# Earlier lists for the experts' middle groups, and a new order of measuring, scaling and routing inside the attention rounds

## The chip, the cores and the metric

The kernel runs on one core of one Trainium2 chip. The metric is the device time of one execution in microseconds (us). An execution's own time is a little longer than the span of its profile, which runs from the first to the last recorded instruction.

## The reference

One layer of a gated cross-attention model, in float32, for 8 batches of 512 rows of 256 numbers:

```python
x = x + tanh(g_xattn) * xattn(layernorm(x), ctx, mask)   # 16 heads of 16
x = x + tanh(g_ffn) * moe(layernorm(x))

# moe, over all 4096 rows
probs = softmax(x @ router_w + router_b)                 # 8 experts
top_w, top_idx = top_k(probs, 2)
output = sum over e: comb[:, e] * (gelu(x @ up[e].T) @ down[e].T)    # 1024 hidden
```

The mask excludes keys. Its rows are all alike here and leave a run of at most 128 adjacent keys, which the kernel finds out at run time before it branches to this variant. Only two of the eight experts count for a row.

## The kernel before

**Engines.** TensorE (PE) multiplies and transposes, VectorE (DVE) reduces and does small arithmetic, ScalarE (ACT) does Exp, Gelu and copies out of PSUM, GpSimd (POOL) issues indirect gathers and scatters, SyncE (SP) issues the other transfers. The code is written as Python functions ("steps") that emit a few instructions each; a scheduler then fixes the order on each engine by its own estimates, except that the instructions marked `tc.keep_in_program_order` ("pinned") stay in the written order among themselves. Each engine, and each engine's queue of transfers, works in that order. An instruction that waits holds what is behind it.

**Start.** The mask and `x` of batch 0 are loaded, batch 0 is measured (`measure`, L211: `look` makes mean and variance of the four 128-row tiles with `bn_stats` and `bn_aggr`, L225 and L228; `settle`, twelve small DVE operations, L233 to L246, makes 1/sqrt of the variance in three Newton steps and the shift). The window of keys is found from the mask; SP loads its start into a register and then issues the windows of context (L508), `x` of batch 1 and the small tensors. `near_i` (L609) is what the branch reads.

**Attention rounds.** The loop at L1198 goes over b = -1 to 7. In round b the attention weights of batch b are computed, the scores' maxima ("tops") of batch b + 1 are found, batch b - 1 is projected, normalized and routed to experts, and batches b + 2 and b + 3 are prepared. A round has four parts g (half of the heads by parity each) of three steps n, and `between(old=b-1, new=b+2, next_=b+3)` (L1114) makes a plan: a list of steps for each (g, n). In order, a part runs `weights_T` (w_ps L1058 on PE, Exp to n_pT L1063 on ACT), then `weigh` of the part before (n_av L1076, DVE raw L1082 and so on), `find_tops` (t_ps L1028 on PE, tops L1033 on DVE), `lower_tops` (top_ps L1046, ql L1047), with the plan's steps between them. The plan's steps that matter here:

- `looks` and `settle` of `measure`, for the rows of the expert part (job "f") and the next batch's attention (job "a").
- `scale` (L275): four ACT operations that make the normalized rows xn_f or xn_a. Only the first of four was pinned. `turn` (L285, L286) transposes them.
- `keys_values` (kv_ps L539, kn L543, nv L544), `keys_T` (k_ps L551, k L557), `keys_less`, `queries` (q_ps L570).
- `logits` (route_ps L323, lgT L328) in the last part of a round. In the next round `route` (L330) transposes lgT (lg_ps L332), adds the bias (L334), and goes on to the softmax, the two best experts and their weights (Exp at L341; both L360). `place` (L363: place_ps L368, then small POOL operations) counts the rows of each expert, and eight `enter` scatters (L398) write a batch's entries into a table in memory.

**Expert groups.** The sorted rows are computed in 32 groups of 256 (and a few beyond). `list_rows(s)` (L800) loads the line of group s into a register on SP and fetches its lists from the table (L806). `load(s)` (L811) issues the expert's weights up (L816) and down (L817), 1024 KB each, into one of three buffers. `fetch(s)` gathers the rows (xg L826), `turn` transposes them, `go_up` does 32 matrix multiplications h_ps (L874) and the Gelus (hT L878), `go_down` 32 of o_ps (L892), and adds to what was gathered of the output (y L895), which POOL scatters back (L898). `SIZES` is [5, 12, 4, 18]: groups 0 to 4 are planned after batch 3's entries, groups 5 to 16 after batch 6's, the rest at the end. Groups 0 to 3 are computed inside rounds 5 to 7 (the table `amid`), groups 4 to 31 in the main loop (`compute`, L914), which runs list_rows(s + 4) and load(s + 2) with group s:

```python
for s in range(DONE, MAIN):
    for step in compute(s, MAIN, DONE):
        step()
        if queue:
            queue.popleft()()
```

`queue` holds what is left of batches 6 and 7: projection, logits, `route`, `place` and scatters. Banks of PSUM: two ("g") for kv_ps, k_ps, q_ps, proj_ps, top_ps, lg_ps, route_ps, place_ps and o_ps, five ("s") for t_ps, w_ps and h_ps, one for n_av.

Of the kernel before, what the change touches and what calls it, by code (L numbers as in the profile page):

```python
# [16 lines left out]
ALU = mybir.AluOpType  # L17
AX = mybir.AxisListType
# [50 lines left out]
def flamingo_layer(ctx: ExitStack, tc: tile.TileContext, a: dict, out: bass.AP):  # L69
# [190 lines left out]
    def shared(p2, small, bank):  # L260
        def layernorms(jobs, pin=False, measured=None):


            said, looks, settle_all = measured or measure(small, [job[:2] for job in jobs], pin)
            settle = lambda pin=False: settle_all(pin)

            def own(k):
                b, which, dst = jobs[k]

                def scale(ts):  # L270
                    if ts[0] == 0:
                        said[k] = p2.tile([P, QT, D], F32, tag="xn", name=f"xn_{which}_{b}")
                    for t in ts:
                        at = k * QT + t
                        ins = nc.scalar.activation(  # L275
                            said[k][:, t, :], xs[b][:, t, :], AF.Identity,
                            bias=said["shift"][:, at : at + 1], scale=said["rstd"][:, at : at + 1],
                        )
                        if t == ts[0] and pin:
                            tc.keep_in_program_order(ins)  # L280

                def turn(c):
                    ps = bank(f"xnT_ps_{which}_{b}_{c}")
                    for t in range(QT):
                        nc.tensor.transpose(ps[:, t * P : (t + 1) * P], said[k][:, t, c * P : (c + 1) * P], ident)  # L285
                    nc.scalar.copy((dst() if callable(dst) else dst)[:, c, :], ps)  # L286
# [14 lines left out]
        def finish(b):  # L301
# [28 lines left out]
            def route():  # L330
                ps = bank(f"lg_ps{b}")[:, :P]
                nc.tensor.transpose(ps, said["lgT"], ident)  # L332
                lg = t3("lg")
                nc.vector.tensor_tensor(  # L334
                    lg, ps.rearrange("p (t e) -> p t e", t=QT)[:, :, :E], over_t(rb), ALU.add
                )
                mx = t2("mx")
                nc.vector.tensor_reduce(mx, lg, AX.X, ALU.max)
                nc.vector.tensor_tensor(lg, lg, over_e(mx), ALU.subtract)
# [64 lines left out]
            places = [place] + [lambda t=t: enter(t) for t in range(b * QT, (b + 1) * QT)]  # L404
            return x2T, keep_x, keep_rows, logits, route, places

# [42 lines left out]
    with early, tc.tile_pool(name="ps_mask", bufs=1, space=PSUM) as ps_mask:  # L449
# [23 lines left out]

        norms_0 = measure(const, [(0, "a")], True)
        settle_0 = norms_0[2]
# [39 lines left out]
        win = load_window(mk, 0)  # L515
        load_x(1, pin=True)
        wins = {1: load_window(const, 1, pin=True)}
# [90 lines left out]
        nc.vector.scalar_tensor_tensor(near, uneven, 0.0, near, ALU.is_le, ALU.mult)  # L608
        tc.keep_in_program_order(nc.vector.tensor_copy(near_i, near))  # L609
        drop = column("drop", P)  # L610
        tc.keep_in_program_order(nc.vector.tensor_scalar(drop, row_ps, -1.0, 1.0, ALU.mult, ALU.add))
# [8 lines left out]

        keep_ones(vals[0])
        for t in vals[1:]:
            keep_ones(t)
# [5 lines left out]
    def experts(pool, seen, half_bank, bank, row_bank):  # L629
# [283 lines left out]

        def compute(s, end, first):  # L914

# [13 lines left out]
            else:  # L929

                steps += up[:2] + last + up[2:]
            if s + 4 < end:
                steps.append(lambda: list_rows(s + 4))
# [34 lines left out]
    def attend_near(att):  # L968
# [136 lines left out]

        def normalize(*jobs):
            looks, settle, each = layernorms(jobs, True)
            for job, own in zip(jobs, each):
                normal[job[:2]] = own
            return looks, settle  # L1110

        def between(old, new, next_):
# [9 lines left out]
            if old is not None:  # L1122
                x2T, keep_x, keep_rows, logits, route, place = finish(old)
                jobs.append((old, "f", x2T))
# [5 lines left out]
            if new is not None:  # L1130
# [4 lines left out]
                if new == 1:  # L1135
                    put(1, 1, *turns)
                    put(2, 1, keys_T)
                    put(3, 1, queries[0])
                    put(3, 2, queries[1], keys_less)
                else:  # L1140
                    put(1, 1, *turns, keys_T)
                    put(3, 0, keys_less)
                    put(2, 0, queries[0])
                    put(2, 1, queries[1])
# [6 lines left out]
            if next_ is not None:  # L1151
                put(*((2, 2) if old is None else (0, 2)), looks[-1])
            if old is not None:
# [4 lines left out]
            if jobs:  # L1158
                put(*((3, 1) if old is None else (1, 2)), settle)
            if old is not None:  # L1160
                put(2, 0, *scales)
                put(2, 2, lambda: keep_rows(rows_f()))
                put(3, 0, *turns)
                put(3, 1, logits)
                place, *enter = place
                counts = [count for count, end in zip(plans, PARTS) if old + 1 == end]
                later.append((route, place, enter, counts))
            return plan


        def begin():
# [75 lines left out]
        wait = lambda: None  # L1247
        (route, place, enter, _), (route_last, last, enter_last, counts) = later
        mixed = [step for pair in zip(rest, [route, place, *enter] + [wait] * len(rest)) for step in pair]
        spread = [step for one in enter_last for step in (one, wait, wait)]  # L1250
        queue = deque([*mixed, route_last, last, *spread, *counts])
        for s in range(DONE, MAIN):
            for step in compute(s, MAIN, DONE):
                step()
# [9 lines left out]
    def attend_anywhere(att):  # L1264
# [143 lines left out]
        def end(b):  # L1408
            x2T, keep_x, keep_rows, logits, route, place = finish(b)
            (look,), settle, ((normal, scales, turns),) = layernorms([(b, "f", x2T)])  # L1410
            return [keep_x, look, settle, *scales, lambda: keep_rows(normal()), *turns, logits, route, *place]

# [178 lines left out]
```

## Time and profile before

| What | us |
|---|---|
| median of 9 executions | 813.44 (812.07 to 818.64) |
| the profiled execution, its own time | 811.85 |
| its span | 810.1 |
| PE busy in the span | 751.5 |
| first w_ps of rounds 0 to 7 | 37.0, 62.05, 98.03, 136.10, 174.80, 213.52, 262.79, 307.40 |
| main loop alone on PE, about | 445 to 777 |

The profile is a record of one execution: for each engine the start and length of each instruction, what its engine waited for before it, and for PE the clock that was granted, as a share of full speed. The mean granted clock was 0.97. A line such as L1033 is a line of the kernel before. In lines of groups, "out<-in" are the names of the tiles that are written and read, with buffer numbers left out, and x16 counts instructions. "[1.59 <-PE row_ps L599]" says that the engine had been idle for 1.59 us and that the PE instruction of line 599 ended this.

### The profile page before, as it was taken

What the parts mean: (1) busy time and instruction counts of PE and PEld (TensorE: products, weight loads), DVE (VectorE), ACT (ScalarE), POOL (GpSimd) and SP (SyncE); (2) the same over time, 40 slices, a digit from 0 to 9 for tenths busy, and PEclk for the clock granted to TensorE, in tenths of its full rate; (3) what the DMA queues carried; (4) which work ended last, traced back from release to release, by engine and by line L of the source; (5) the groups of instructions that cost most, each with busy time, mean ns of one, the idle gap of its engine ahead of it and who ended that gap; (6) DMA issues with size and microseconds to landing.
All of it is one profiled execution on the core that took longest, in us unless ns stands there. A gap on an engine that the chain in (4) does not pass through costs nothing. (4 is left out here: it accounts for less than half of the span.)

```text
span 810.1 us, 11155 instructions
## 1 busy us (share of the span) xinstructions
PE 751.5 (93%) x3898; PEld 541.1 (67%) x3898; DVE 409.7 (51%) x1315; ACT 254.9 (31%) x487; POOL 312.0 (39%) x420
## 2 busy tenths in 40 slices
PE   8999987888999989998899999999999999999992
PEld 3444443434565756667678888888788788888872
DVE  8887895959664574533163353525343433523300
ACT  4563735454554434332312111111211211121110
POOL 2021115142627251546573534444443443344331
PEclk9998998999899999999999999999999999999997
DMA  5700201000573230143638566666744754654310
GB/s 163 265 7 8 78 34 56 27 30 28 193 263 121 81 121 14 54 158 115 227 125 294 192 215 219 204 224 192 243 164 152 227 195 151 203 202 174 100 53 25
DMA packets 82728, 113.32 MB, mean 140 GB/s; under 512 B 16605, under 2 KB 67552, under 8 KB 82656
## 3 DMA queue, kind: packets, MB, share of 16 engines
q1 hardware_dynamic: 70000, 85.16, 31.3%
q0 software_dynamic: 11840, 26.76, 9.9%
q8 instruction: 35, 0.57, 0.3%
q10 hardware_dynamic: 816, 0.53, 0.2%
q14 instruction: 37, 0.30, 0.1%
HBM read 92.66 MB, written 20.28 MB: 139 GB/s over the span
## 5 line engine op out<-in xcount | busy, mean ns | idle before, releaser
L892 PE MATMUL o_ps<-down,hT 128*128 128x256 f32 x1088 | 243.0, 381 | 4.3 <-DVE y L895 4.3
L874 PE MATMUL h_ps<-xT,up 128*128 128x256 f32 (+1 forms) x1024 | 242.7, 393 | 4.0 <-DVE xT L851 2.4
L892 PEld LDWEIGHTS o_ps<-down,hT 128*128 128x128 f32 x1088 | 205.8, 190 | 40.7 <-DVE y L895 6.3
L874 PEld LDWEIGHTS h_ps<-xT,up 128*128 128x128 f32 x1024 | 193.2, 190 | 46.7 <-issue 5.6
L863 DVE STREAM_TRANSPOSE xT<-xg 32x128 f32<-32x128 f32 (+1 forms) x368 | 115.6, 314 | 180.0 <-DMA xg<-rows,listed 165.0
L878 ACT ACTIVATE hT<-h_ps 128x512 f32<-128x512 f32 (+1 forms) x144 | 82.1, 573 | 347.7 <-PE h_ps L874 302.3
L898 POOL DMA_INDIRECT out<-y,listed x68 | 68.5, 1007 | 149.8 <-DVE y L895 131.4
L826 POOL DMA_INDIRECT y<-out,listed x68 | 64.9, 955 | 76.5 <-DMA out<-y,listed 49.4
L1033 DVE TENSOR_REDUCE tops<-t_ps 128x4 f32<-128x512 f32 x128 | 79.5, 683 | 20.5 <-PE t_ps L1028 17.1
L1063 ACT ACTIVATE n_pT<-w_ps 128x512 f32<-128x512 f32 x128 | 67.8, 597 | 48.5 <-PE w_ps L1058 45.1
L826 POOL DMA_INDIRECT xg<-rows,listed x68 | 66.1, 972 | 37.9 <-issue 18.6
L398 POOL DMA_INDIRECT table<-entries,place_i x64 | 63.0, 985 | 25.0 <-issue 16.5
L895 DVE SCALAR_TENSOR_TENSOR y<-o_ps,listed,y 128x256 f32<-128x256 f32 x68 | 31.3, 482 | 74.4 <-PE o_ps L892 50.2
L1058 PE MATMUL w_ps<-ql,km 32*128 32x512 f32 x256 | 52.7, 685 | 1.8 <-DVE tops L1033 1.4
L1010 POOL TENSOR_TENSOR x<-x,bo 128x1024 f32<-128x1024 f32 x8 | 18.8, 2354 | 72.4 <-DVE bo L1009 42.4
L1028 PE MATMUL t_ps<-k,q 32*128 32x256 f32 x512 | 44.5, 420 | 1.3 <-ACT n_pT L1063 0.9
L1082 DVE STREAM_TRANSPOSE raw<-n_av 128x512 f32<-128x512 f32 x32 | 22.8, 712 | 45.1 <-PE n_av L1076 28.3
L1028 PEld LDWEIGHTS t_ps<-k,q 32*128 32x128 f32 x512 | 27.4, 192 | 22.2 <-issue 8.2
L1076 PE MATMUL n_av<-n_pT,nv 128*32 128x512 f32 x256 | 38.7, 680 | 1.2 <-DVE xT L851 1.1
L1097 PE MATMUL proj_ps<-woT,oT 128*128 128x256 f32 x128 | 32.6, 397 | 0.0
L570 PE MATMUL q_ps<-n_xnT,wqT 128*128 128x512 f32 x64 | 31.4, 615 | 0.9 <-ACT n_xnT L286 0.6
L1097 PEld LDWEIGHTS proj_ps<-woT,oT 128*128 128x128 f32 x128 | 24.2, 196 | 9.7 <-issue 3.1
(220 smaller groups left out, 527.1 us busy)
## 6 DMA issues: line engine op xcount, KB each, us to landing
up<-in_upT SPq DMA_DIRECT2D x32, 1024.0 KB
down<-in_downT SPq DMA_DIRECT2D x32, 1024.0 KB
out<-x SPq DMA_DIRECT2D x8, 512.0 KB
rows<-xn_f SPq DMA_DIRECT2D x8, 512.0 KB
x<-in_x SPq DMA_DIRECT2D x7, 512.0 KB
table<-none SPq DMA_DIRECT2D x1, 2400.0 KB
xg<-rows,listed POOLq DMA_INDIRECT x68
y<-out,listed POOLq DMA_INDIRECT x68
```

Of the source, the lines that this page charges most:

```text
L398: nc.gpsimd.indirect_dma_start(out=table_parts[2 * t + i][:, :], out_offset=bass.IndirectOffsetOnAxis(ap=place_i[:, t, i : i + 1], axis=0) ...
L826: ins = nc.gpsimd.indirect_dma_start(out=dst, out_offset=None, in_=src[: seen[JOBS[s][0]], :], in_offset=bass.IndirectOffsetOnAxis(ap=list ...
L863: nc.vector.transpose(dst[32 * g : 32 * g + 32, i], src[32 * i : 32 * i + 32, g])
L874: nc.tensor.matmul(ps[:, i, :], lhsT=up[:, dc, (f + i) * P : (f + i + 1) * P], rhs=xT[:, dc, :], start=(dc == 0), stop=(dc == DC - 1),)
L878: nc.scalar.activation(made[s][:, f : f + m, :], ps, AF.Gelu)
L892: nc.tensor.matmul(ps, lhsT=hT[:, f, h * P : (h + 1) * P], rhs=down[:, f, :], start=(f == 0), stop=(f == FC - 1))
L898: ins = nc.gpsimd.indirect_dma_start(out=out_parts[h][:, :], out_offset=bass.IndirectOffsetOnAxis(ap=listed[:, n, h, 0:1], axis=0), in_=y[ ...
L1028: ins = nc.tensor.matmul(ps[j][:, u], lhsT=q[rows_j, c, t * P : (t + 1) * P], rhs=k[rows_j, c], start=True, stop=True)
L1033: nc.vector.tensor_reduce(top[:, 2 * tp : 2 * tp + 2, :].rearrange("p t (i x) -> p t i x", i=2)[:, :, :, 32 * j], ps[j], AX.X, ALU.max,)
L1058: ins = nc.tensor.matmul(ps[j], lhsT=km[rows_j, c, i, :], rhs=lowered[b, c][rows_j, i, :], start=True, stop=True)
L1063: nc.scalar.activation(pT[:, j, :], ps[j], AF.Exp)
L1097: nc.tensor.matmul(ps[:, t - ts[0], :], lhsT=outs[b, c][:, t * P : (t + 1) * P], rhs=w["woT"][:, c, :], start=(c == 0), stop=(c == DC - 1),)
```

## The change

It has six parts.

1. `x` of batch 1 is loaded before SP reads the window's start. Batch 1 is measured with batch 0's functions: its `look` stands right after `near_i`, its `settle` after the first `keep_ones`. It was measured at the begin of the rounds.
2. In round 0 the measurement of batch 3 goes from step (2, 2) to (1, 2), its `settle` from (3, 1) to (2, 0). In later rounds both stay where they were.
3. All four scalings of a job are pinned, not the first alone.
4. `route` is cut in two. The transpose and the addition stay in `route`, which goes from step (0, 2) to (0, 0); `choose`, the rest, stays at (0, 2), and its maximum is pinned.
5. `keys_T` goes from step (1, 1) to (1, 2).
6. The lists of groups 8 to 16 are asked for in the last step of round 7, after those of groups 6 and 7, and `compute` skips them; `turn_rows(4)` is moved one step by it.

```diff
@@ scale
-                        if t == ts[0] and pin:
+                        if pin:
                             tc.keep_in_program_order(ins)
@@ finish
             def route():
                 ps = bank(f"lg_ps{b}")[:, :P]
                 nc.tensor.transpose(ps, said["lgT"], ident)
-                lg = t3("lg")
+                said["lg"] = t3("lg")
                 nc.vector.tensor_tensor(
-                    lg, ps.rearrange("p (t e) -> p t e", t=QT)[:, :, :E], over_t(rb), ALU.add
-                )
+                    said["lg"], ps.rearrange("p (t e) -> p t e", t=QT)[:, :, :E], over_t(rb), ALU.add
+                )
+
+            def choose():
+                lg = said["lg"]
                 mx = t2("mx")
-                nc.vector.tensor_reduce(mx, lg, AX.X, ALU.max)
+                tc.keep_in_program_order(nc.vector.tensor_reduce(mx, lg, AX.X, ALU.max))
                 nc.vector.tensor_tensor(lg, lg, over_e(mx), ALU.subtract)
...
@@ start
-        norms_0 = measure(const, [(0, "a")], True)
+        load_x(1, pin=True)
+        norms_0, norms_1 = (measure(const, [(b, "a")], True) for b in range(2))
...
         win = load_window(mk, 0)
-        load_x(1, pin=True)
...
         tc.keep_in_program_order(nc.vector.tensor_copy(near_i, near))
+        norms_1[1][0]()
...
         keep_ones(vals[0])
+        norms_1[2](True)
         for t in vals[1:]:
@@ compute
-            if s + 4 < end:
+            if listed <= s + 4 < end:
                 steps.append(lambda: list_rows(s + 4))
@@ between
-                    put(1, 1, *turns, keys_T)
+                    put(1, 1, *turns)
+                    put(1, 2, keys_T)
...
-                put(*((2, 2) if old is None else (0, 2)), looks[-1])
+                put(*((1, 2) if old is None else (0, 2)), looks[-1])
...
-                put(*((3, 1) if old is None else (1, 2)), settle)
+                put(*((2, 0) if old is None else (1, 2)), settle)
@@ amid
-            + [lambda: load(5), lambda: turn_rows(4), lambda: list_rows(6), lambda: list_rows(7)],
+            + [lambda: load(5), lambda: turn_rows(4), lambda: [list_rows(s) for s in range(6, LISTED)]],
         }
         DONE = 4
+        LISTED = SIZES[0] + SIZES[1]
@@ the rounds
-        looks, settle = normalize((1, "a", lambda: xnT[1]))
-        for step in (*looks, settle):
-            step()
+        normalize((1, "a", lambda: xnT[1]), measured=norms_1)
...
-            for route, place, enter, counts in behind_route:
-                plan[0, 2].append(route)
+            for route, choose, place, enter, counts in behind_route:
+                plan[0, 0].append(route)
+                plan[0, 2].append(choose)
                 plan[1, 2].append(place)
@@ the main loop
-            for step in compute(s, MAIN, DONE):
+            for step in compute(s, MAIN, DONE, LISTED):
```

In the main loop `route` and `choose` of batches 6 and 7 are still run as one step.

More of the change, by code (lines that the diff above doesn't have):

```diff
@@ L404, in finish @@
             places = [place] + [lambda t=t: enter(t) for t in range(b * QT, (b + 1) * QT)]
-            return x2T, keep_x, keep_rows, logits, route, places
+            return x2T, keep_x, keep_rows, logits, route, choose, places
         return layernorms, finish
@@ L912, in downs, with compute @@
             return [lambda h=h: go_down(s, h) for h in range(halves(s))]
-        def compute(s, end, first):
+        def compute(s, end, first, listed=0):
             steps = [lambda: fetch(s + 2)] if s + 2 < end else []
@@ L1104, in attend_near, with normalize @@
         normal = {}
-        def normalize(*jobs):
-            looks, settle, each = layernorms(jobs, True)
+        def normalize(*jobs, measured=None):
+            looks, settle, each = layernorms(jobs, True, measured)
             for job, own in zip(jobs, each):
@@ L1122, in between @@
             if old is not None:
-                x2T, keep_x, keep_rows, logits, route, place = finish(old)
+                x2T, keep_x, keep_rows, logits, route, choose, place = finish(old)
                 jobs.append((old, "f", x2T))
@@ L1166, in between @@
                 counts = [count for count, end in zip(plans, PARTS) if old + 1 == end]
-                later.append((route, place, enter, counts))
+                later.append((route, choose, place, enter, counts))
             return plan
@@ L1247, in attend_near, with choice @@
         wait = lambda: None
-        (route, place, enter, _), (route_last, last, enter_last, counts) = later
-        mixed = [step for pair in zip(rest, [route, place, *enter] + [wait] * len(rest)) for step in pair]
+        (route, choose, place, enter, _), (route_last, choose_last, last, enter_last, counts) = later
+        def choice(route, choose):
+            route()
+            choose()
+        first = [lambda: choice(route, choose), place, *enter]
+        mixed = [step for pair in zip(rest, first + [wait] * len(rest)) for step in pair]
         spread = [step for one in enter_last for step in (one, wait, wait)]
-        queue = deque([*mixed, route_last, last, *spread, *counts])
+        queue = deque([*mixed, lambda: choice(route_last, choose_last), last, *spread, *counts])
         for s in range(DONE, MAIN):
-            for step in compute(s, MAIN, DONE):
+            for step in compute(s, MAIN, DONE, LISTED):
                 step()
@@ L1408, in end @@
         def end(b):
-            x2T, keep_x, keep_rows, logits, route, place = finish(b)
+            x2T, keep_x, keep_rows, logits, route, choose, place = finish(b)
             (look,), settle, ((normal, scales, turns),) = layernorms([(b, "f", x2T)])
-            return [keep_x, look, settle, *scales, lambda: keep_rows(normal()), *turns, logits, route, *place]
+            return [keep_x, look, settle, *scales, lambda: keep_rows(normal()), *turns, logits, route, choose, *place]
         def scores(b, h, t):
```

## The prediction

> **What bounds the kernel now.** I read the page first: busy shares, then the slices.
>
> ```profile
> PE 751.5 (93%) x3898; PEld 541.1 (67%) x3898; DVE 409.7 (51%) x1315; ACT 254.9 (31%) x487; POOL 312.0 (39%) x420
> ...
> PE   8999987888999989998899999999999999999992
> ...
> DVE  8887895959664574533163353525343433523300
> ```
>
> PE is the bound: 751.5 of 810.1 us. A slice is 20.25 us; the eighteen-odd slices up to about 373 us are the rounds of attention, with VectorE (DVE) at 7 to 9 in the first six; from there on PE is at 8 or 9 and DVE at 1 to 5. So the end can come sooner only by the 58.6 us in which PE is idle, or by stretches at half clock. Next, the busy times by stage (columns: stretch, its length, then busy time and instructions of PE, PEld, DVE, ACT, POOL; PE clock, DMA share, GB/s):
>
> ```profile
> 65.40:72.20 6.80, 6.80 (x16) 2.06 (x15) 3.71 (x7) 1.79 (x3) 1.03 (x1) 0.50 0.01 2
> 143.30:162.20 18.90, 15.47 (x103) 8.48 (x107) 17.85 (x67) 7.62 (x18) 4.10 (x15) 1.00 0.08 29
> ...
> 445.00:777.00 332.00, 328.07 (x1464) 277.79 (x1465) 128.36 (x386) 56.01 (x99) 141.00 (x145) 1.00 0.56 188
> ```
>
> From 445 on PE is busy 328.07 of 332.00: whatever the change does must be won before. Inside a round (143 to 162) DVE is busy 17.85 of 18.90 and PE 15.47, so a PE wait taken away there mostly comes back behind DVE. The first row is a stretch at half clock. Last, PE's own waits, by what ended them (columns: us in total, times, longest):
>
> ```profile
> PE route_ps L323 <- ACT x2T L286: 7.4, 3, 3.6
> PE o_ps L892 <- DVE y L895: 4.3, 5, 1.3
> PE lg_ps L332 <- DVE x L1102: 4.2, 4, 1.8
> ...
> PE h_ps L874 <- DMA up<-in_upT: 1.7, 1, 1.7
> ...
> PE w_ps L1058 <- DVE tops L1033: 1.4, 1, 1.4
> ```
>
> The change goes for rows three to five: 4.2 + 1.7 + 1.4 = 7.3 us that PE shows as idle, and for DVE work at the start.
>
> **Part 1, batch 1 measured sooner.** Before the first tops (L1033) can be reduced, DVE runs batch 1's eight statistics (18.66 to 21.6) and twelve settling operations of 0.16 us (21.67 to 24.0):
>
> ```profile
> 17.02 0.29 DVE L611 TENSOR_SCALAR drop<-row_ps 128x128 f32<-128x128 f32 x1 [1.59 <-PE row_ps L599]
> ...
> 21.38 0.17 DVE L681 TENSOR_SCALAR line<-iota_e 128x9 f32<-128x9 f32 x1 [1.10 <-DMA rw<-in_rw]
> ...
> 23.92 0.69 DVE L1033 TENSOR_REDUCE tops<-t_ps 128x4 f32<-128x512 f32 x1
> ```
>
> The statistics cost 3 x 0.40 + 0.35 + 0.2, about 1.8 us, and go into the idle 1.59 ahead of L611; the load of x1 is issued on SP ahead of the register load of the window, some 7 us sooner, when the data queues are empty. That leaves +0.2 at L611, and the settling (2.3) after `keep_ones`, where the statistics were. It ends near 21.5 instead of 24.0. The first scores (t_ps, 21.52, 1.15 us) have their first bank by about 22.1, so L1033 starts 1.8 sooner. PE has kv_ps (22.60, 1.98 us) between the two lots of scores, which eats part of it. I take **-1.4** (0 if kv_ps sets the pace, -1.9 if not). The branch operand `near_i` still comes first, at 15.28.
>
> **Part 2, batch 3 measured sooner.** Its statistics and settling are 58.40 to 62.5, 4.1 us of DVE right ahead of raw (62.43) and the tops at 63.87, for which PE waits 1.44. Moved to about 51, they find 1.35 us idle ahead of raw (52.35) and 0.69 ahead of L1033 (55.29): 4.1 - 2.04 = 2.1 us push that L1033 to about 57.3, and PE, which wanted its tops at 57.03, idles some 2 us there. After it DVE has 4.1 less to do and the last tops start at about 62.6 instead of 63.87. **-1.3**. It is -4.7 if the half clock of 65.4 to 72.2 (6.8 at 0.50 costs 3.4), which followed the 1.44, goes too, and +0.5 if the new idle time costs more. I take no clock gain, since a new gap of 2 us stands in for the old one.
>
> **Part 3, logits turned at the begin of a round; keys a step later; scalings pinned.** The transpose lg_ps and the addition out of it move from step (0,2) to (0,0), right behind kv_ps. The PE waits at lg_ps are 0.80, 0.80, 0.79 in the rounds that begin at 98, 136 and 175, and 1.84 in that at 213.5. In the first three DVE is busy 94% (row two above), and the two waits that the pinned scalings free (t_ps behind n_pT, 0.45 and 0.47) lie under the same DVE: I take a quarter, -0.2 each, **-0.6** (0 to -3.3). In the round at 213.5 PE is busy 38.16 of 40.00 and DVE 25.66, so more of the 1.84 stays: **-1.0** (0 to -1.84). The keys a step later let place_ps wait for k (it waits 0.75 to 0.85 already), about +0.6, under DVE's tops: nothing; without that cover +0.6 in each of three rounds, which moves the upper bound of these rounds to +1.8. The waits at route_ps (7.4) stay.
>
> **Part 4, the router's Exp among the Gelus.** `choose` is now pinned by its maximum only, and in the rounds at 262.8 and 307.4 ScalarE's (ACT's) order puts the router's Exp between the first and the second h_ps of groups 1 and 2. Gelu and Exp need different tables; a load there and one back, in two rounds: four loads more. A load is 1.283 us in the trace, 5.1 in all. Beside them:
>
> ```profile
> 274.38 0.60 ACT L878 ACTIVATE hT<-h_ps 128x512 f32<-128x512 f32 x1 [2.89 <-PE h_ps L874]
> ...
> 317.24 0.60 ACT L878 ACTIVATE hT<-h_ps 128x512 f32<-128x512 f32 x1 [3.30 <-PE h_ps L874]
> ```
>
> ACT is idle 2.89 and 3.30 there; 2 x 1.28 + 0.23 (the Exp) = 2.8 just fits, but the Exp must also wait for DVE's logits, which come at about 274.0, behind ql. Behind it stand the next Gelu and with it a bank of the five that h_ps and w_ps share: I get the w_ps bank 0.3 us late in each round. **+0.6** (0 to +5.1).
>
> The Trainium skill, "ScalarE: Activation LUTs", section "What ACT_TABLE_LOAD costs", speaks against this part: 1283 ns for the load and 1380 ns of drain for every switch, 2.66 us. Four switches and two Exps would be 11.1 us against 6.2 idle, +4.9 in place of +0.6, and the whole sum would end 4.3 higher. This trace has the load's 1283 but no row for a drain: at 319.58 a load begins with the end of the Gelu before it, and the Exp begins 1.30 later.
>
> **Part 5, lists of groups 8 to 16 in the last round.** In the last step of the last round SP now issues nine lists more, behind those of groups 6 and 7 (352.84). Before, each was issued in its group's turn, behind scatters into the table (L398) that it must not overtake, and SP's queue, in order, held the weights behind it:
>
> ```profile
> SPq L806 <- DMA table<-entries,place_i: 14.9, 3, 10.0
> ```
>
> List 8 went at 379.81 and up6 at 380.74; list 9 at 392.48 and up7 at 394.50; list 10 so:
>
> ```profile
> 417.69 0.37 SPq L806 DMA_DIRECT2D listed<-table  x1
> 419.02 0.00 SPq L816 DMA_DIRECT2D up<-in_upT  x1
> ```
>
> PE then idled 1.68 for up8 (422.01). Without the lists, up8 can go when its buffer is free: the h_ps of group 5 end at 380.7, so about 382. POOL's scatters in turn waited 5.0 for these list reads (3.17 at 381.72, 1.86 at 419.72); they come sooner, and so do the gathers of y behind them, for which PE waits 0.71 at 444.65. **-2.4** (1.68 + 0.7). Nine lists at 0.4 to 0.6 us of queue are about 4.5 us, before up6 is due, with list 6 ahead of them, so the rows of group 6 wait no longer than now. Bounds: 0 if the hidden waits of 390 to 428 take it back, -4.7 if the 2.31 at lg_ps (392.72) goes as well.
>
> **Sum:** -1.4 - 1.3 - 0.6 - 1.0 + 0.6 - 2.4 = -6.1. The profiled execution took 811.85 (span 810.1), so about 805.8; it lies 1.6 under the median of 813.44, and the median becomes **807.3**.
>
> **Rivals.** (a) *The clock comes back too.* Two of the seven half-clock stretches ahead of 373 us lie right behind gaps that go (65.4 to 72.2 behind 1.44, 225.8 to 229.2 behind 1.84): 3.4 + 1.7, so -6.1 - 5.1 gives 802; with a third, about 799. For it: each followed a gap of at least 0.7. Against: gaps of 1.19 at 112.9, 152.4 and 190.6 were followed by none, and part 2 makes a new gap.
>
> The Trainium skill, "TensorE: Matmul & The Clock Gate", section "HAM oscillation — how this bites in real kernels", asks for idle gaps above some 3.4 us; by it none of the removed gaps had cost clock and this case would give nothing over the sum. The row disagrees: 0.50 from 65.4 on behind a gap of 1.44.
>
> (b) *The rounds do not get shorter.* DVE is full in rounds 0 to 4, so what PE gains at one step it waits at the next; only half of the lists' term and of the start remain, and the loads: -1.2 - 0.7 + 0.6 = -1.3, near 812.
>
> (c) *Slower: the Exp holds the Gelus.* Place: ACT in the rounds at 262.8 and 307.4. If DVE's logits come after about 274.4, or the two loads pass the idle 2.89 and 3.30, the Gelu behind them is late by the excess, and PE, out of shared banks, idles. From a gap of 1.44 on a half-clock stretch can follow. Price: 2 x (2.6 + 3.4) = 12, the sum then +5.9, so 819.3. For it: logits arrive within 0.4 us of the limit. Against: ACT is busy 20.53 of 50 us from 250 on and 22.16 of 50 from 300 on, so it has time to catch up.
>
> **Chances.** A measurement of this kernel tells 0.3% from no change, 2.4 us: faster is below 811.0, slower above 815.9. Forecast (803.5 to 811) 0.46; (a) 798 to 803.5, 0.16; below that 0.03; (b) 811 to 815.9, 0.16; (c) 815.9 to 821, 0.16, above 0.03. Faster 0.65, same 0.16, slower 0.19. The bounds of the parts add up to -16.4 and +7.4 (797.0 to 820.8). The range leaves out what is below 798 and the upper part of (c): 798 to 817.
>
> **What would show it.** The first L1033 at about 22.1; w_ps of the first round about 1.4 sooner; a gap near 57 and none at 63; no PE wait at lg_ps in the rounds at 98 to 213; four more table loads on ACT (L878 six to about eight, the router's too), with hT idle times under 3; lists together at about 353 to 358, no wait of SP for the scatters, up8 near 382 and no PE wait for up. I am wrong if PE waits for hT or w_ps banks at 275 and 318, if new half-clock stretches come, or if the weights come sooner and PE waits for y instead.

## The result and the profile after

The changed kernel takes 818.49 us (median of 20, 813.27 to 824.33) where the kernel before, run beside it, takes 813.93 (median of 62): ratio 1.0064, interval 1.0048 to 1.0079. It is slower by 0.64%; the forecast was 807.3, the range 798 to 817. The profiled execution has a span of 817.0 against 810.1.

Of the page after, the lines that answer to those of before, and the clock (tenths granted in each slice):

```profile
PE 753.1 (92%) x3898; PEld 545.2 (67%) x3898; DVE 409.2 (50%) x1315; ACT 262.2 (32%) x491; POOL 313.2 (38%) x420
...
PE   8999988888898989998699999999999999999992
...
DVE  8798885868564575532144434534433423523300
...
PEclk9999997987998999999799999999999999999997
```

The clock of before:

```profile
PEclk9998998999899999999999999999999999999997
```

PE is busy 1.6 us longer and idle 5.3 us longer. ACT has four instructions more (491 against 487): the table loads that were foreseen. To place the loss, I took the first n_av of each round from the two timelines:

| round | 0 | 1 | 2 | 3 | 4 | 5 | 6 | 7 | end of the span |
|---|---|---|---|---|---|---|---|---|---|
| before | 44.97 | 77.33 | 108.28 | 147.75 | 185.97 | 225.47 | 277.18 | 320.04 | 810.1 |
| after | 43.16 | 71.03 | 100.98 | 142.16 | 181.32 | 224.42 | 278.44 | 320.50 | 817.0 |
| after - before | -1.8 | -6.3 | -7.3 | -5.6 | -4.7 | -1.1 | +1.3 | +0.5 | +6.9 |

The start and rounds 0 and 1 win 7.3 us, rounds 2 to 5 lose all of it, and 6.4 more are lost between round 7 and the end. That last loss lies ahead of the steady part, in busy times by stage (columns as in the prediction; the first row is of before, the others of after):

```profile
320.00:445.00 125.00, 115.84 (x582) 92.33 (x578) 49.85 (x230) 37.24 (x66) 64.81 (x99) 0.99 0.48 156
```

```profile
320.50:452.00 131.50, 118.01 (x579) 94.64 (x578) 48.26 (x212) 37.07 (x65) 64.74 (x98) 0.95 0.46 152
452.00:784.00 332.00, 328.19 (x1465) 278.21 (x1466) 128.52 (x387) 56.27 (x99) 141.71 (x145) 1.00 0.56 187
```

The stage up to the steady part is 6.5 us longer for the same work, at a clock of 0.95 in place of 0.99. PE is busy only 2.2 us longer in it (118.01 against 115.84), so the lower clock is the smaller part of this loss and idle time, 4.3 us, the larger. The steady part, 332 us with 328 busy, is unchanged. PE's waits after:

```profile
PE x_ps L854 <- DVE raw L1087: 6.1, 2, 3.7
PE xnT_ps_a L285 <- DVE x L1107: 5.5, 3, 1.8
PE place_ps L371 <- ACT k L560: 4.9, 3, 1.7
PE h_ps L879 <- DVE xT L856: 4.8, 3, 2.6
PE route_ps L323 <- issue: 4.4, 3, 1.7
PE route_ps L323 <- ACT x2T L286: 4.3, 2, 2.3
...
PE h_ps L879 <- issue: 3.6, 5, 1.0
```

Of before:

```profile
PE xnT_ps_a L285 <- DVE x L1102: 3.6, 3, 1.2
...
PE place_ps L368 <- ACT k L557: 2.3, 3, 0.8
```

The three rows that the change went for (lg_ps behind x, up, w_ps behind tops) are gone. In their place stand longer waits at xnT_ps_a and place_ps (and at x_ps, 6.1 against 4.2), and two rows that before did not have: "issue", in which PE waits for nothing that the profile shows. Of half clock the trace has 51.2 us ahead of the tail, against 37.5 before; at 0.50 that is up to 6.8 us of work lost, as far as PE had work in it.

PE's timeline of group 6, where one of these rows comes from, and GpSimd's (POOL) at that time:

```profile
392.43 1.78 PE L879 MATMUL h_ps<-xT,up 128*128 128x256 f32 x7
394.94 0.67 PE L879 MATMUL h_ps<-xT,up 128*128 128x256 f32 x2 [0.73 <-issue]
396.34 0.38 PE L879 MATMUL h_ps<-xT,up 128*128 128x256 f32 x1 [0.73 <-issue]
...
399.87 1.11 PE L879 MATMUL h_ps<-xT,up 128*128 128x256 f32 x3 [1.03 <-issue]
403.21 0.47 PE L332 MATMUL lg_ps<-ident,lgT 128*128 128x128 f32 x1 [2.23 <-ACT lgT L328]
```

```profile
381.33 1.08 POOL L401 DMA_INDIRECT table<-entries,place_i  x1 [0.92 <-DMA up<-in_upT]
382.71 0.97 POOL L401 DMA_INDIRECT table<-entries,place_i  x1 [0.30 <-issue]
...
397.99 1.01 POOL L903 DMA_INDIRECT out<-y,listed  x1 [0.30 <-issue]
401.24 0.99 POOL L831 DMA_INDIRECT y<-out,listed  x1 [2.24 <-DMA out<-y,listed]
```

In the kernel before, 16 h_ps of this group take 3.62 us, 0.22 us each; here nine take from 394.9 to 401.0, in steps of some 0.7 us. ACT and DVE too start late on banks that PE has long filled (lgT at 402.89 behind a route_ps that ended at 392.50). I call this a **slow stretch**. It lies in the time in which POOL issues indirect transfers 0.30 us apart, 14 of them from 381.33 to 399.0. In the kernel before, the same run was broken by a wait of 3.17 (for the list) and one of 2.03, and the slow stretch ended near 395:

```profile
381.72 0.96 POOL L398 DMA_INDIRECT table<-entries,place_i  x1 [3.17 <-DMA listed<-table]
...
394.93 0.97 POOL L826 DMA_INDIRECT xg<-rows,listed  x1 [2.03 <-remote]
```

```profile
395.03 0.33 PE L332 MATMUL lg_ps<-ident,lgT 128*128 128x128 f32 x1 [2.31 <-ACT lgT L328]
395.19 3.62 PE L874 MATMUL h_ps<-xT,up 128*128 128x256 f32 x16
```

### The profile page after: what moved, and what is told of

It reads as the page before. It is cut to its first block, busy times and chain, and to the rows that moved or that the text cites. A ratio compares the mean times of both kernels' runs of the same rounds, so it can differ in the third digit from the quotient of the medians.

```text
span 817.0 us, 11151 instructions
## 1 busy us (share of the span) xinstructions
PE 753.1 (92%) x3898; PEld 545.2 (67%) x3898; DVE 409.2 (50%) x1315; ACT 262.2 (32%) x491; POOL 313.2 (38%) x420
## 5 line engine op out<-in xcount | busy, mean ns | idle before, releaser
L879 PE MATMUL h_ps<-xT,up 128*128 128x256 f32 (+1 forms) x1024 | 247.9, 398 | 8.3 <-DVE xT L856 4.8
L879 PEld LDWEIGHTS h_ps<-xT,up 128*128 128x128 f32 x1024 | 195.9, 193 | 52.6 <-issue 7.9
L1038 DVE TENSOR_REDUCE tops<-t_ps 128x4 f32<-128x512 f32 x128 | 79.4, 684 | 25.5 <-PE t_ps L1033 14.1
L1033 PE MATMUL t_ps<-k,q 32*128 32x256 f32 x512 | 40.5, 415 | 0.4 <-ACT k L560 0.4
L1081 PE MATMUL n_av<-n_pT,nv 128*32 128x512 f32 x256 | 36.7, 647 | 2.7 <-DVE xT L856 2.7
L1033 PEld LDWEIGHTS t_ps<-k,q 32*128 32x128 f32 x512 | 25.4, 189 | 17.2 <-issue 12.2
```

The source lines that it names most:

```text
L879: nc.tensor.matmul(ps[:, i, :], lhsT=up[:, dc, (f + i) * P : (f + i + 1) * P], rhs=xT[:, dc, :], start=(dc == 0), stop=(dc == DC - 1),)
L1033: ins = nc.tensor.matmul(ps[j][:, u], lhsT=q[rows_j, c, t * P : (t + 1) * P], rhs=k[rows_j, c], start=True, stop=True)
L1038: nc.vector.tensor_reduce(top[:, 2 * tp : 2 * tp + 2, :].rearrange("p t (i x) -> p t i x", i=2)[:, :, :, 32 * j], ps[j], AX.X, ALU.max,)
```

## The experiments

Parts are numbered here as in the section on the change. The chips differ. On two of the five that the runs came to, the kernel before takes 814 us and has slow stretches in each round from 2 on; on three it takes 792 to 793, and in the runs traced there, some of which have the rounds of before, the rounds show none. The table gives ratios to the kernel before on the same chip. The chip of the result was of the first kind (all its times of before lie above 810).

| kernel | chips with slow stretches | chips without |
|---|---|---|
| changed kernel | 1.0064 [1.0048, 1.0079] | 0.9966 [0.9946, 0.9986] |
| before + part 6 (lists) | 1.0071 [1.0045, 1.0096] | 0.9968 [0.9953, 0.9983] |
| before + parts 1, 2 (measuring) | 0.9952 [0.9931, 0.9972] | |
| before + part 5 (keys) | | 1.0031 [1.0015, 1.0047] |
| changed - part 6 | 1.0006 [0.9990, 1.0022] | |
| changed - part 5 | 1.0002 [0.9981, 1.0023] | |
| changed - parts 5, 6 | 0.9922 [0.9899, 0.9945] | 0.9933 [0.9907, 0.9959]; 0.9928 [0.9909, 0.9947] |
| the same, weights ahead of lists | | 0.9871 [0.9849, 0.9893] |

**First set: parts alone and parts undone**, all on a chip with slow stretches. The lists alone:

```diff
-            if s + 4 < end:
+            if listed <= s + 4 < end:
...
-            + [lambda: load(5), lambda: turn_rows(4), lambda: list_rows(6), lambda: list_rows(7)],
+            + [lambda: load(5), lambda: turn_rows(4), lambda: [list_rows(s) for s in range(6, LISTED)]],
```

> The kernel before with part 6 alone (lists of groups 8 to 16 asked for in round 7). Theory A, from the changed kernel's trace, where the stretch from the first n_av of round 7 to the first waiting o_ps behind 440 grew from 124.6 to 131.3 us: the early lists cost 6.7, so about 820. Theory B: that stretch is lost to an accident of the clock and the lists bring what was forecast, 1 to 2.4 less, so about 812. Theory C, everything is lost in the rounds by the new order of logits and keys: no difference here, 814.

819.23 us against 813.78, as theory A has it. Up to round 7 its trace keeps the times of before within 0.6 us (first n_av of round 7 at 320.40), so nothing in the rounds is needed for this loss. Group 6 of this run:

```profile
391.30:403.10 11.80, 6.64 (x33) 3.94 (x32) 0.00 (x0) 2.05 (x5) 6.86 (x7) 0.87 0.51 191
```

PE is busy 6.64 of 11.80 us, DVE does nothing, POOL is issuing all along.

Parts 1 and 2 alone (batch 1 measured at the start, batch 3 in steps (1,2) and (2,0)):

> The kernel before with parts 1 and 2 alone (batches 1 and 3 measured sooner). In the changed kernel's trace the first n_av of round 1 comes 6.3 us sooner and that of round 2 7.3 sooner. Theory A and C: these two parts keep most of this, 807 to 809. Theory B (rounds 2 to 4 wait for DVE, so that nothing gained ahead of them lasts): 812 to 814.

809.24, 0.48% faster: the gain of the start lasts.

The changed kernel with the lists in turn again, and with `put(1, 1, *turns, keys_T)` again:

> The changed kernel without part 6 (lists asked for in each group's turn, as before). Theory A: 818.5 - 6.7, about 812. Theory B: 1 to 2 slower than the changed kernel, 820. Theory C: 818.

> The changed kernel without part 5 (keys_T again in step (1,1)). In rounds 2 to 4 of the changed kernel PE waits 4.9 us at place_ps for k, against 2.3 before, and 5.5 at xnT_ps_a against 3.6. Theory C: these waits bring the half-clock stretches of the rounds; 4 to 6 less, about 813. Theory A: the rounds are bound by DVE, 0 to 2 less, 817 to 818.

813.73 and 814.68, ratios 1.0006 and 1.0002. So each of the two parts costs about 0.6% beside the others, theory A and theory C each are right about their half, and neither alone is the cause.

**Second set: the scatters.** This set ran on a chip without slow stretches. The write of rows moved:

```diff
-                put(2, 2, lambda: keep_rows(rows_f()))
                 put(3, 0, *turns)
                 put(3, 1, logits)
+                put(3, 2, lambda: keep_rows(rows_f()))
```

> The kernel before with one step moved: the write of a batch's normalized rows to memory (rows<-xn_f) goes from step (2,2) to (3,2), behind the eight scatters into the table of its round. Theory S: PE, ACT and DVE run slow in every round from about 2 us after that write is issued until the eighth scatter has been issued, so the write among the scatters is what starts it; apart, the slow stretches (127 to 134, 166 to 173, 252 to 258, 297 to 302 before) and the route_ps waits of 7.4 us go, with some of the half clock behind them: 795 to 806. Theory P: the scatters alone, issued back to back, do it, whatever is written beside them: no change, 812 to 815. Theory D: DVE bounds these rounds and the slow stretch is only seen because PE has nothing else: no change, 812 to 815.

791.79 against 792.29 (0.9987 [0.9974, 1.0001]); it tells nothing of theory S, since there were no slow stretches to take away.

> The changed kernel without parts 5 and 6. If the parts add up, 818.5 less 3.8 (keys) less 4.8 (lists): 810, and what is left of parts 3 and 4 against batches 1 and 3 measured sooner alone (809.2) is nothing. If the gain of the keys is only the stretch of 370 to 450 falling out otherwise (its half clock was 10.2 us there, as in the changed kernel), 813 to 814. If turning the logits sooner pays once the keys do not hold back the places: 806 to 807.

786.19 against 792.29, ratio 0.9933: on this chip as the parts add up.

The scatters of batch 6 left out, with the lists early and in turn:

```diff
+        enter = [wait] * len(enter)
         mixed = [step for pair in zip(rest, [route, place, *enter] + [wait] * len(rest)) for step in pair]
```

> The kernel before with the lists early (part 6) and without the eight scatters of batch 6, so the groups from 17 on miss its rows. Theory S or P for the lists: without the wait for list 8, GpSimd issues 16 transfers without a pause from 380 to 402, and the engines are slow from 391 to 403; without the eight scatters the 32 h_ps of group 6 take 7 to 9 us instead of 15.6, and the whole is 5 to 9 less than with the lists alone: 810 to 814. Theory L: the weights of groups 7 and 8, that come at 388 to 395, hold the engines; no change, 817 to 820.

> The kernel before without the eight scatters of batch 6, lists in turn as before; groups from 17 on miss its rows. Theory S or P: what the lists cost is the unbroken run of GpSimd, so without these scatters early lists and lists in turn differ by less than 2 us: 810 to 814, as the run with early lists. Theory L: early lists stay 4 to 6 slower, so this one is at 812 to 814 and the other at 817 to 820.

Both leave out batch 6's entries, so the later groups lack its rows. 785.28 and 782.58: here early lists stay 2.7 us slower, which is a hint of theory L on such a chip and no more, as the four executions of each overlap (782.87 to 787.59, 781.28 to 785.33) and with the scatters the lists gain on such a chip (0.9968). Both are 7 to 10 us faster than before although nothing was slow: leaving out the scatters saves time by itself. What this set showed instead is the chip. In round 2 `no_scatter6` has the instructions of before; PE's route_ps in before (first kind of chip) and in this run:

```profile
132.97 0.43 PE L323 MATMUL route_ps<-x2T,rw 128*32 128x128 f32 x8 [2.71 <-ACT x2T L286]
134.47 0.66 PE L323 MATMUL route_ps<-x2T,rw 128*32 128x128 f32 x8 [1.07 <-ACT x2T L286]
```

```profile
130.86 0.91 PE L323 MATMUL route_ps<-x2T,rw 128*32 128x128 f32 x16 [0.36 <-ACT x2T L286]
```

The scatters of that round run from 122.2 to 132.5 and from 122.6 to 132.6. On the one chip PE and ACT come back with their end; on the other nothing is held. From round 2 to round 3 it is 39.46 us against 33.52.

**Third set: the change on a chip without slow stretches.**

> The changed kernel, unaltered, beside the ones below on one chip. The kernel before took 813.8 us on one chip and 792.3 on another, on which no trace shows the slow stretches during the scatters. Theory S (the change loses by these stretches): on a chip with them 1.006 times before; on one without them faster than before, 0.992 to 0.997. Theory W (the lists and the keys cost by their own waits): 1.002 to 1.006 on both.

790.03 against 792.63, ratio 0.9966: **faster**, as theory S said.

> The kernel before with part 6 alone, once more. On a chip with slow stretches 1.007 times before, as measured. On one without: theory S 0.997 to 1.000, since up8 comes sooner (the wait of 1.7) and nothing is slow; theory W 1.003 to 1.007, as the first pair of runs without batch 6's scatters hints (785.3 with early lists, 782.6 in turn).

790.45, 0.9968: the lists' sign turns over too, and theory W falls for them. Why they bring only 2.5 us there is in PE's waits of the changed kernel on this chip, and of the one without parts 5 and 6:

```profile
PE o_ps L897 <- DVE y L900: 11.9, 5, 5.8
PE xnT_ps_a L285 <- DVE x L1107: 5.4, 3, 1.8
PE place_ps L371 <- ACT k L560: 4.9, 3, 1.7
```

```profile
PE h_ps L879 <- DMA up<-in_upT: 9.0, 2, 6.2
PE xnT_ps_a L285 <- DVE x L1107: 5.0, 3, 1.8
PE o_ps L897 <- DVE y L900: 4.2, 4, 1.5
PE place_ps L371 <- ACT k L560: 2.2, 3, 0.8
```

The wait for the weights (9.0) is gone, and the wait for y, whose gathers stand behind the scatters on POOL, has grown from 4.2 to 11.9. The lists alone do the same: no wait for up, and 10.2 for y, where `rows_late`, with the lists in turn, waits 4.2 for up and 4.3 for y.

> The changed kernel without parts 5 and 6, once more. It was 0.993 times before on the chip without slow stretches. On one with them, if the parts add up, 0.994 to 0.996; if the keys' gain there was the accident of 370 to 450, 0.999 to 1.001.

> The kernel of the run above with the write rows<-xn_f moved behind the scatters, from step (2,2) to (3,2). On a chip with slow stretches, theory S says that this write among the scatters starts them: they go, and the time is 12 to 18 us less than that of the run above. If the scatters alone do it: the same. On a chip without slow stretches: the same.

785.90 (0.9928) and 785.43 (0.9918 [0.9898, 0.9938]): the gain without parts 5 and 6 is there again, the later write makes no difference.

**Fourth set: again on a chip with slow stretches.**

> The kernel before with rows<-xn_f written behind the scatters, once more. On a chip with slow stretches (before at about 814): theory S, the write among the scatters starts them, 798 to 806; theory P, the scatters alone do it, 812 to 815. On a chip without (before at about 792): no change, as measured.

816.41 against 814.60, ratio 1.0028 [1.0002, 1.0053]: no gain. The trace shows that the scheduler had moved the write in one round only, from 203.3 to 222.6; in the others it was issued within 1 us of where it had been, once 3 us later. So the test holds for that round alone. There the scatters run from 198.6 to 208.7 with no such write beside them, and still:

```profile
210.89 1.14 PE L323 MATMUL route_ps<-x2T,rw 128*32 128x128 f32 x16 [2.56 <-ACT x2T L286]
```

PE waits until 2 us behind the last scatter. In one round, then, the write is not what starts the slow stretch, which speaks for theory P.

> Early lists, batch 6's eight scatters left out (groups from 17 on miss its rows), once more. On a chip with slow stretches: if the lists lose there by the unbroken run of scatters and gathers (380 to 402), h_ps of group 6 take under 10 us instead of 15.6, and the time is within 2 us of the next run; if by the early weights, 4 to 6 above the next run. On a chip without: 2 to 3 above the next run, as measured.

> Lists in turn, batch 6's eight scatters left out, once more: the partner of the run above. On a chip with slow stretches some 5 to 10 under before (the slow stretch of 390 to 395 and what waits behind the scatters goes); on one without 0.988 times before, as measured.

807.32 and 808.68, ratios 0.9911 [0.9889, 0.9933] and 0.9913 [0.9881, 0.9945]: without batch 6's scatters early lists cost nothing on such a chip. Group 6 with early lists and without these scatters:

```profile
388.73 3.19 PE L874 MATMUL h_ps<-xT,up 128*128 128x256 f32 x14
391.85 0.64 PE L323 MATMUL route_ps<-x2T,rw 128*32 128x128 f32 x16
392.42 3.72 PE L874 MATMUL h_ps<-xT,up 128*128 128x256 f32 x16
395.98 0.27 PE L332 MATMUL lg_ps<-ident,lgT 128*128 128x128 f32 x1
```

The 16 h_ps that took from 395.2 to 403.1 with the scatters take 3.72 us, and SP issues up8 at 388.50 here and at 388.40 there. So early weights by themselves are not the cause; it takes the scatters. Nor are weights needed: round 2 has its slow stretch before the first of them is issued (212.68). That the missing pause, and not scatters beside early weights, lengthens it in group 6 is read from the runs of POOL; no run took the weights and the pause apart.

> The changed kernel without parts 5 and 6, on whatever chip this is. On one with slow stretches: 0.994 to 0.996 times before if the parts add up, 0.999 to 1.001 if not. On one without: 0.993, as measured twice.

807.41 against 814.60, 0.9922: it gains on both kinds of chip.

**Fifth set**, on a chip without slow stretches. `keys_T` a step later, alone:

> The kernel before with part 5 alone (keys_T a step later). Differences of other runs put this part at +5 to +7 us (no_lists against best_3, keys_back against the changed kernel). Theory K, the part costs by itself, since PE waits at place_ps for k (4.9 in place of 2.3 in three rounds), the scatters start later and each wait of 1.6 or more is followed by half clock: 1.005 to 1.008 times before, on either kind of chip. Theory M, it costs only beside the logits turned sooner, which take PE's banks and DVE at that place: 0.999 to 1.002.

794.74 against 792.71, 1.0031 [1.0015, 1.0047]. The part costs by itself, 2.5 us, less than theory K said. PE's waits at place_ps grow by 0.85 us in each of three rounds (1.69, 1.60, 1.60 against 0.85, 0.75, 0.75 in before), 2.55 in all, about the same. The single execution does not share the loss out like that: from the first n_av of round 2 to that of round 5 it is 34.52, 33.55 and 39.03 us, against 33.52, 33.48 and 36.68 in `no_scatter6`, which has before's rounds (3.4 more). The half clock that theory K expected behind each of these waits did not come: none of the three was followed by any. Beside parts 3 and 4 the three rounds take 34.56, 35.23 and 40.70 against 33.38, 33.06 and 37.67, 6.4 more, which looks like a share of theory M. But `best_load_first`, the last run below, takes 34.59, 34.34 and 37.95 without part 5, 2.8 more than the run without parts 5 and 6 above, in rounds of the same program. So single executions scatter too much to show the share. By the medians, parts 5 and 6 together cost 4.1 us on one such chip (790.03 against 785.90), where the one alone costs 2.5 and the other alone gains 2.2; what makes them dearer beside the rest stays open.

Last, the weights ahead of the lists, from the changed kernel without parts 5 and 6:

```diff
+            if s + 2 < end:
+                steps.append(lambda: load(s + 2))
             if s + 4 < end:
                 steps.append(lambda: list_rows(s + 4))
-            if s + 2 < end:
-                steps.append(lambda: load(s + 2))
```

> The changed kernel without parts 5 and 6, and with the two lines of the main loop exchanged, so that a group's weights are asked for ahead of the list of the group four on. PE waited 3.9 and 1.9 us for up in the run of best_3 and 6.2 and 2.8 on the other kind of chip, since SP held the weights behind the lists that wait for the scatters; GpSimd's pause for the lists stays. If that wait is what costs: 3 to 6 less than 0.992 to 0.993 times before, so 0.985 to 0.989. If, as with early lists, the gathers of y behind the scatters are late next: 0.991 to 0.994.

782.22 against 792.71: 0.9871 [0.9849, 0.9893], the best version, and free of the wait for up. y is late next here too, but with 9.0 us in place of 11.9:

```profile
PE o_ps L897 <- DVE y L900: 9.0, 5, 5.0
PE xnT_ps_a L285 <- DVE x L1107: 5.5, 3, 1.8
PE x_ps L854 <- DMA xg<-rows,listed: 2.2, 2, 2.0
PE place_ps L371 <- ACT k L560: 1.2, 3, 0.5
```

It was not run on a chip with slow stretches.

## Why the prediction was wrong, point by point

**Parts 1 and 2 of the prediction** were right in place and a little small: -2.7 forecast, -3.9 measured (0.48%). The first tops (L1033, now L1038) came at 22.68, not at 22.1. The gap of 2 us that was to appear near 57 did not: the statistics found room at 48.87 to 52.9, the next tops began at 55.07, and with the gap at 63 the half clock of 65.4 to 72.2 went as well. That is the other end of the term, -4.7, and the larger part of the table's -6.3 at round 1 of the profiled execution. It was no accident of one execution: all ten traces with the gap of 1.44 have half clock there, beginning between 64.0 and 66.9, and of the ten without the gap one has. So "I take no clock gain" is what made this term small, and rival (a) was right about this stretch.

**Part 3 of the prediction, "the keys a step later ... under DVE's tops: nothing"** is the first step that failed: put at nothing, it cost 2.5 us alone, on a chip without slow stretches, and about 5 beside the other parts on one with them (1.0064 against 1.0002). I had argued from DVE's 94% that a PE wait there costs nothing. On a chip without slow stretches, PE in the changed kernel and in that without parts 5 and 6:

```profile
109.51 0.71 PE L554 MATMUL k_ps<-pick,kn 128*128 128x128 f32 x4 [0.24 <-ACT n_xnT L286]
111.91 0.38 PE L371 MATMUL place_ps<-both,before 128*128 128x32 f32 x2 [1.69 <-ACT k L560]
```

```profile
108.99 0.66 PE L1051 MATMUL top_ps<-ident,tops 128*128 128x128 f32 x4 [0.23 <-ACT n_xnT L286]
110.50 0.38 PE L371 MATMUL place_ps<-both,before 128*128 128x32 f32 x2 [0.84 <-ACT k L560]
```

place_ps needs a bank that k holds until ACT has read it; with k_ps behind top_ps PE waits 0.85 us longer for the bank, about the +0.6 that I had put under cover. The cover is not there: three times 0.85 is 2.55, and the part alone cost 2.5. Behind place_ps stand w_ps and n_av, and eight scatters on POOL. In this execution half clock came behind it as well:

```profile
113.60:117.00 3.40, 3.40 (x10) 0.91 (x11) 2.91 (x12) 2.06 (x4) 2.19 (x11) 0.50 0.00 0
```

That this is a price of the part is not shown. Of the eight waits of 1.6 to 1.7 at place_ps that lie outside half clock, in four traces with the part, this one alone was followed by any within 4 us. The run's next two stretches, from 144.3 and 178.5, came behind waits of 1.81 at xnT_ps_a, which the kernels without part 5 have too. And ahead of the tail this run has 30.7 us of half clock, while three traces whose rounds are those without the part have 13.7, 13.7 and 23.9. The Trainium skill, "TensorE: Matmul & The Clock Gate", section "HAM oscillation — how this bites in real kernels", asks for gaps above some 3.4 us; in this row 0.50 stands behind a gap of 1.69, and in round 0 behind one of 1.44. With the lists beside it or without, the keys (part 5 of the change) cost 0.6 to 0.8% on a chip with slow stretches (1.0064 against 1.0002, 1.0006 against 0.9922). The scatters start later there, 15.0 to 16.6 us behind the first n_av of rounds 2 to 4 (`after`, `no_lists`) against 14.1 to 15.0 without part 5 (`keys_back`, `best_3`), and the slow stretches with them; that this makes the rest of the price is argued, not shown.

**Part 5 of the prediction, the lists: "-2.4 ... Bounds: 0 ..., -4.7"**, is the second. Measured: +5.5 (819.23 - 813.78). The path to up8 was right in the main: up8 left SP at 388.51 (not 382, as it stood behind down7), still 30 us sooner than before, and the wait of 1.68 for up went. What failed is "POOL's scatters in turn waited 5.0 for these list reads; they come sooner", counted as a gain. That wait was a pause in a run of indirect transfers, and on this chip the engines stay slow until shortly behind the end of the run: 391 to 403 instead of 390 to 395. On a chip without slow stretches the lists gained 2.2 us, near the -2.4, but there the last sign of "I am wrong if" came true: PE waited for y instead, 10.2 us. My own record of slow stretches near the scatters, "the hidden waits of 390 to 428", was used as a bound at 0 and not beyond. The nine lists took 1.03 us of SP each (11 in 11.32 us from 353.84), not 0.4 to 0.6; no wait is traced to that.

**Part 4 of the prediction** happened as written: the Exp waited 1.53 us for DVE's logits, between two loads.

```profile
272.39 1.28 ACT L344 ACT_TABLE_LOAD   x1
275.20 0.23 ACT L344 ACTIVATE pr<-lg 128x32 f32<-128x32 f32 x1 [1.53 <-DVE lg L342]
275.45 1.28 ACT L883 ACT_TABLE_LOAD   x1
276.74 1.25 ACT L883 ACTIVATE hT<-h_ps 128x512 f32<-128x512 f32 x2
```

Rival (c) said that this would cost 12 us; it named the time (819.3) nearly and the cause wrongly, as the kernel without parts 5 and 6 has the same loads and is 0.8% faster than before. No cost of them shows: from the first n_av of round 5 to that of round 7 its trace takes 86.0 us on a chip without slow stretches, against 87.5 in `no_scatter6`, which has four loads less. The Trainium skill's drain of 1380 ns for a switch ("ScalarE: Activation LUTs", "What ACT_TABLE_LOAD costs") is not in these rows: the Gelu starts 1.29 us behind the start of its load.

**The logits and the pinned scalings** (-1.6 forecast) were not run alone. The difference between 0.9922 (parts 1 to 4) and 0.9952 (parts 1 and 2), from two sets, is 2.4 us, within the sum of both intervals. The waits at lg_ps went, as forecast, but those at xnT_ps_a became longer, 1.6 to 1.8 us instead of 1.2 in each of three rounds, in all nine traces that have parts 3 and 4. The sum had no term for this.

**Added up.** Parts 1 and 2 -3.9, logits and scalings about -2.4, lists +5.5, keys about +5 make some +4, and the change measured +5.2 (0.64%).

**Rival (b)** had it that rounds do not get shorter behind the start; rounds 2 to 5 did give the gain back, but by part 5 of the change, since parts 1 to 4 keep it. For rival (a) I had said that "each followed a gap of at least 0.7"; of the seven stretches this holds for five, as the trace of before has no such gap ahead of the half clock of 300.9 and of 345.3.

**What stays open:** why the engines are slow on some chips while POOL issues transfers without a pause. The trace has no releaser for it, and the write of rows could be excluded in one round only. Whether it is the lack of a pause or the number of transfers that counts was not varied by itself.

## What to carry to other kernels

A wait that goes is also a pause that goes: ask what the engine behind it does without it, and what runs beside that. A moved step is priced by all that stands behind it in its queue, down to the slowest follower, not by the cover over its own wait. And where a loss comes with hidden stalls, measure on more than one chip before a change of half a per cent is kept or dropped.

## What the runs showed of the hardware

The same program took 814 us on two chips and 792 on three, 2.6% apart, with granted clocks of 0.97 and 0.98. The difference lies in the rounds with scatters (39.5 against 33.5 us for round 2), not in the main loop: from the first n_av of round 7 to the end it is 490.1 us in before and 490.4 in `rows_late` on the other kind. On the first kind of chip, PE took about 0.7 us for an h_ps instead of 0.22 while GpSimd issued 14 indirect transfers without a pause, and in round 2 PE and ACT stood still up to the end of eight of them (ACT came back at 132.34, the eight ended at 132.5); the sign of a change of 0.6% turned over between the two kinds. Half clock of 3.4 to 10.2 us began behind idle gaps of PE far shorter than itself, but not behind every one: behind that of 1.44 in round 0 in ten of ten traces, within 4 us behind those of 1.6 to 1.8 at xnT_ps_a in 12 of 27 and behind those of 1.6 to 1.7 at place_ps in one of eight; and some began with no gap of 0.7 ahead of them (300.9 and 345.3 in before).
